# Layer 0 of a four-layer convolution kernel worked on pairs of columns, with the image laid out beforehand

## The chip, the cores and the metric

The kernel runs on one core of one Trainium2 chip, in one launch. The metric is device time in microseconds; three runs of the kernel before gave a median of 11783.54 us. One further execution was profiled, and all views below come from it. TensorE (PE, with PEld for its weight loads), VectorE (DVE), ScalarE (ACT), GpSimd (POOL) and SyncE (SP) work side by side, each through its own instructions in order. GpSimd and SyncE issue the DMAs here.

## The reference

The input `x` is 32 images of 8 channels and 256 x 256 pixels, f32. Each of four layers adds to `x` a function of its group norm (four groups of two channels). Layer 0 is by far the largest:

```python
drive = x[:, :C_OUT]                       # x here is the normalized image
grid = drive
for _ in range(15):
    mapped = 3.9 * grid * (1.0 - grid)
    local = _conv(mapped, K_local, groups=8)            # 3x3, channel by channel
    physics = 0.7 * mapped + 0.3 * local
    grid = 0.85 * physics + 0.15 * drive
cml_out = clip(grid, 0.0001, 1.0 - 0.0001)
h = relu(_conv(x, Wp, bp))                              # 3x3, 8 -> 128 channels
nca_out = sigmoid(_conv(h, Wu, bu))                     # 1x1, 128 -> 8
gin = concatenate([x, cml_out, nca_out], axis=1)        # 24 channels
g = sigmoid(_conv(relu(_conv(gin, Wg1, bg1)), Wg2, bg2))  # 3x3, 24 -> 8; 1x1, 8 -> 8
return g * cml_out + (1.0 - g) * nca_out
```

Layer 1 is a 3x3 convolution of the quantized norm, layer 2 a 3x3 convolution, layer 3 a 5x5 box filter per channel.

## The kernel before, in words

Layer 0 runs over all images first and leaves its result in DRAM (`x1_d`). Layers 1 to 3 follow in a second part, image by image.

For each image b, layer 0 has four streams of work.

`errands(b)` loads the image, takes its statistics (`bn_stats`), normalizes it in place on VectorE, stores it to a DRAM buffer with borders (`xn_d`), and loads it again in two layouts for the map (`xa`, `xb`). The other streams also read `xn_d`.

`steps(b)` is the map, the loop of 15 steps. The image lies in `state` as strips of 32 rows on 32 partitions, 4 x 36 of them, each half an image wide (130 columns with overlap). A step has three jobs s. A job is `products` (L528): for each of the three horizontal taps dx, 16 small products of a 32x32 weight with 32 x 390 columns, one for every 32x32 tile of the array, so three rounds of 16. The vertical taps and the mapped value are in the weights `wm_sb`. A job fills four of the eight PSUM banks. `take` (L543, VectorE) adds the drive and writes the new state back; a square on ScalarE (L608) makes the mapped value, since 3.9 g (1 - g) is a constant minus 3.9 (g - 0.5)^2. Every second step the layout of the strips changes sides between channel and strip, and the weights follow it. A strip has 28 rows of its own and two spare ones at each end, so rows must be passed between strips every second step: `exchange` copies columns on VectorE (L558) and issues four DMAs on SyncE for each of two groups p (L389, state<-state). The result goes to `cm_d` with DMAs of GpSimd (L385, cm_d<-xb). L482 is the square that starts an image's map, once for each p.

`hidden(n)`, four blocks n per image, is the wide convolution: eight jobs of three rounds of four products, 32 rows by 128 columns of weights over 512 columns (L690), from tiles `zx` that GpSimd loads. Each job fills four banks, which ScalarE (L697) and VectorE (L702) drain with a relu, `SHARE` = 1024 of 2048 columns on ScalarE. Two "seconds" (L725) bring 128 channels back to 8, and a sigmoid follows (L740).

`gate(n)` has three pieces (L809), for `zx`, `zc` (from `cm_d`) and `zn` (from `nn_d`): each is three rounds, one per dx, of eight products 64 x 32 over 512 columns. A 1x1 product (L837), a sigmoid and four tensor operations on VectorE close it.

The order of all this is not the order of the text. `Plan` collects the operations with a cost, a rank and a due time (`due=b + (3 * k + s) / 45` for the map, `b + LAG + ...` for hidden and gate, `LAG` = 0.6 of an image), plays them through, hands out PSUM banks through `Hold(count)`, and then emits them; each engine executes its own list in that order. So the hidden products of image b run beside the later steps of its own map and the first steps of the next one.

Of the kernel before, what the change touches and what calls it, by code (L numbers as in the profile page):

```python
# [10 lines left out]
F32 = mybir.dt.float32  # L11
# [12 lines left out]
HP, WP = H + 2, W + 2  # L24
NPX = RB * W
NCH = NPX // 512
RC = C * WP

STEPS = 15
HOP = 28  # L30
# [5 lines left out]
WT = 130  # L36
OF = 126
# [4 lines left out]
RATE = 200.0  # L42
# [4 lines left out]
SHARE = 1024  # L47
# [3 lines left out]
PAIRS = ((0,), (0, 1), (1,))  # L51
# [22 lines left out]
class Plan:  # L74
# [17 lines left out]
    def run(self):  # L92
# [33 lines left out]
        def begin(e, t):  # L126
# [25 lines left out]
            if op.size:  # L152
                moved = max(moved, t + cost) + op.size / RATE
                done = moved + HOP_US
# [40 lines left out]

def window(ap, offset, dims):
    return bass.AP(ap.tensor, ap.offset + offset, [list(d) for d in dims])
# [3 lines left out]
def kernel(  # L201
    ctx, tc, x, wm, kern, kera, eye32, wp, bp, wu, bu, wg1, bg1, wg2, bg2, w1, b1, w2, self2, near2,
    taps2, b2, w3, self3, taps3, eye, gavr, gsel, out,
):
    nc = tc.nc
    B = x.shape[0]
# [18 lines left out]
    x1_d = [dram.tile([P, NPX], F32, name=f"x1_d{b}") for b in range(B)]  # L225
    x3_d = [dram.tile([C, H, W], F32, name=f"x3_d{b}") for b in range(2)]
# [66 lines left out]
    with ExitStack() as es:  # L293
# [12 lines left out]
        wm_sb = const(wt, wm, [P, 10, 3, 32], "wm_sb")  # L306
        kern_sb = const(wt, kern, [P, 36, 9], "kern_sb")
        kera_sb = const(wt, kera, [P, 6, 9], "kera_sb")
        eye32_sb = const(wt, eye32, [P, 32], "eye32_sb")
# [4 lines left out]
        wg1_sb = const(wt, wg1, [P, 3, 3, 32], "wg1_sb")  # L314
# [4 lines left out]
        flat = wm_sb.rearrange("p c t m -> p (c t m)")  # L319
        nc.vector.tensor_scalar(flat, flat, -R_ * (1.0 - BETA_) * EPS_, None, ALU.mult)  # L320
        for c in range(10):
            nc.vector.scalar_tensor_tensor(
                wm_sb[:, c, 1, :], eye32_sb, -R_ * (1.0 - BETA_) * (1.0 - EPS_), wm_sb[:, c, 1, :],
                ALU.mult, ALU.add,
            )
        lift = wt.tile([P, 36], F32, name="lift")
        lifta = wt.tile([P, 6], F32, name="lifta")
        for t, k in ((lift, kern_sb), (lifta, kera_sb)):
            nc.vector.tensor_reduce(t, k, AX.X, ALU.add)
            nc.vector.tensor_scalar(  # L330
                t, t, 0.25 * R_ * (1.0 - BETA_) * EPS_, 0.25 * R_ * (1.0 - BETA_) * (1.0 - EPS_),
                ALU.mult, ALU.add,
            )
        minus = wt.tile([P, 1], F32, name="minus")
        nc.vector.memset(minus, -0.5)
        mean_sb = wt.tile([P, P], F32, name="mean_sb")
        nc.vector.memset(mean_sb, 1.0 / P)
# [3 lines left out]

        xbs = [wt.tile([P, 36, WT], F32, name=f"xb{i}") for i in range(2)]
        xa = wt.tile([P, 36, WT], F32, name="xa")
        state = wt.tile([P, 36, WT + 2], F32, name="state")
        nc.gpsimd.memset(state, 0.25)
        zero = wt.tile([P, 32], F32, name="zero")
        nc.vector.memset(zero, 0.0)  # L350


        xn_d = [dram.tile([HP, C, WP], F32, name=f"xn_d{i}") for i in range(3)]
        cm_d = [dram.tile([HP, C, WP], F32, name=f"cm_d{i}") for i in range(3)]
        nn_d = [dram.tile([HP, C, WP], F32, name=f"nn_d{i}") for i in range(3)]
        for t in (*xn_d, *cm_d, *nn_d):
            nc.sync.dma_start(window(t, 0, [[24, RC // 24], [1, 24]]), zero[0 : RC // 24, 0:24])
            nc.sync.dma_start(
                window(t, (HP - 1) * RC - 24, [[24, RC // 24 + 1], [1, 24]]),
                zero[0 : RC // 24 + 1, 0:24],  # L360
            )
            nc.sync.dma_start(
                window(t, RC - 1, [[16 * WP, P], [WP, 16], [1, 2]]),
                zero.rearrange("p (a b) -> p a b", b=2),
            )
# [4 lines left out]
        def part_of(xb, s):  # L370

            j, h = divmod(s, 2)
            whole = xb.rearrange("p s w -> p (s w)")[32 * j : 32 * j + 32, 0 : 2 * C * W]
            return whole.rearrange("p (c h w) -> p c h w", h=2, w=W)[:, :, h]

        def strips(q, s, i):


            p, u = divmod(4 * s + q, 6)
            h, v = divmod(u, 3)  # L380
            return HOP * (3 * v + i), p, h

        def pool_dma(to, src, after, size, rank=1):
            return add(
                "POOL", 0.6, lambda: nc.gpsimd.dma_start(to(), src()), after, rank, size=size  # L385
            )

        def sp_dma(to, src, after, rank=0):
            return add("SP", 0.58, lambda: nc.sync.dma_start(to(), src()), after, rank)  # L389


        stored_cm, stored_xn, free_a, free_s = {}, {}, {}, {}
        drive_b, drive_a, begun = {}, {}, {}
        zx_read, stored_nn = {}, {}

        def errands(b):

            xb, s = xbs[b % 2], {}
            plain = xb.rearrange("p s w -> p (s w)")
            old = stored_cm.get(b - 2, []) + [begun[key] for key in ((b - 1, 1),) if key in begun]  # L400
            loads = [
                pool_dma(
                    lambda i=i: part_of(xb, i),
                    lambda i=i: window(
                        x, b * C * H * W + 32 * i * W, [[W, 32], [H * W, C], [1, W]]
                    ),
                    old, 262,
                )
                for i in range(8)
            ]  # L410
            bns = []
            for c in range(C):
                def do(c=c):
                    if c == 0:
                        s["bn"] = small.tile([P, C, 6], F32, name="bn0")
                    nc.vector.bn_stats(s["bn"][:, c, :], plain[:, bass.ts(c, 512)])

                bns.append(add("DVE", 0.7, do, loads + bns[:1], 2))

            def join():  # L420
                s["mv"] = small.tile([P, 4, 2], F32, name="mv0")
                s["mean"] = small.tile([P, 4], F32, name="mean0")
                s["rstd"] = small.tile([P, 4], F32, name="rstd0")
                for g in range(4):
                    nc.vector.bn_aggr(
                        s["mv"][:, g], s["bn"][:, 2 * g : 2 * g + 2].rearrange("p a b -> p (a b)")
                    )
# [3 lines left out]
                add, slot, lambda: s["mv"], 4, lambda: s["mean"], lambda: s["rstd"], mean_sb, [a]  # L431
            )
            norms = [
                add(
                    "DVE", 0.8,
                    lambda g=g: nc.vector.tensor_scalar(
                        plain[:, bass.ts(g, 1024)], plain[:, bass.ts(g, 1024)],
                        s["mean"][:, g : g + 1], s["rstd"][:, g : g + 1], ALU.subtract, ALU.mult,
                    ),
                    [a], 2,  # L440
                )
                for g in range(4)
            ]
            old = [o for n in range(4 * (b - 3), 4 * (b - 2)) for o in zx_read.get(n, [])]
            stored_xn[b] = [
                pool_dma(
                    lambda i=i: window(
                        xn_d[b % 3], (1 + 32 * i) * RC + 1, [[RC, 32], [WP, C], [1, W]]
                    ),
                    lambda i=i: part_of(xb, i),  # L450
                    norms + old, 262,
                )
                for i in range(8)
            ]
            def queue(n):

                def sized(to, src, after, size):
                    return add(
                        "SP", 0.58, lambda: nc.sync.dma_start(to(), src()), after, 1, size=size
                    )  # L460

                return sized if b == 0 and n % 2 else pool_dma


            for p in range(2):
                loads = [
                    queue(h)(
                        lambda i=i, h=h, p=p: xa[
                            32 * i : 32 * i + 32, 18 * p + 9 * h : 18 * p + 9 * h + 9
                        ],  # L470
                        lambda i=i, h=h, p=p: window(
                            xn_d[b % 3], RC + (2 * i + p) * WP + OF * h + 1,
                            [[RC, 32], [HOP * RC, 9], [1, WT]],
                        ),
                        stored_xn[b] + free_a.get((b - 1, p), []), 150,
                    )
                    for i in range(4) for h in range(2)
                ]
                mine = slice(18 * p, 18 * p + 18)
                begun[b, p] = add(  # L480
                    "ACT", 2.25,
# [54 lines left out]
        def job(s):  # L536
            return slice(12 * s, 12 * s + 12)
# [41 lines left out]
        def steps(b):  # L579

            old = {s: [begun[b, p] for p in PAIRS[s]] for s in range(3)}
            for k in range(STEPS):
# [32 lines left out]
                elif k % 2:  # L615
                    got = [exchange(p, [squares[p], squares[p + 1]]) for p in range(2)]
                    for s in range(3):
                        for p in PAIRS[s]:
                            old[s] = old[s] + got[p]
# [913 lines left out]
```

## Time and profile before

| | us |
|---|---|
| median of 3 runs (lowest to highest) | 11783.54 (11780.98 to 11790.86) |
| profiled execution, its own time | 11818.99 |
| its span, first to last instruction | 11816.9 |
| first start of a map (L482) | 78.9 |
| layer 0 ends, about | 9948 |
| busy: PE / PEld | 10696.8 / 4839.0 |
| busy: DVE / ACT / POOL | 6725.5 / 4961.2 / 3791.6 |

A line of a group reads: source line, engine, operation, out<-in by the program's names, shapes, count | busy time and mean ns of one | idle time of the engine just before them, and what ended most of it. "PE bank" in the chain is TensorE writing PSUM. The granted clock is the share of full speed that the throttle gave TensorE; over the whole execution it was 0.954.

### The profile page before, as it was taken

To read this page: it belongs to the slowest core of one execution; us is meant where nothing else is said; L and a number is where in the kernel's file an instruction comes from. 1 tells how busy PE (TensorE), PEld (TensorE's weight loads), DVE (VectorE), ACT (ScalarE), POOL (GpSimd) and SP (SyncE) were. 2 spreads that over 40 slices of the span, in tenths; PEclk is the share of its full clock that TensorE was granted. 3 is DMA by queue.
4 is the path that set the end of the run, shared out by engine and by line. 5 is a ranking of instruction groups with operands and counts; after the bars stand their busy time and mean duration, and the time that the engine had idled before them with its cause. 6 is when DMAs were issued, how large, how long until landed. Compare 5 with 4: busy or idle time off the path is not lost.

```text
span 11816.9 us, 453849 instructions
## 1 busy us (share of the span) xinstructions
PE 10696.8 (91%) x210376; PEld 4839.0 (41%) x210376; DVE 6725.5 (57%) x9864; ACT 4961.2 (42%) x4254; POOL 3791.6 (32%) x6448
## 2 busy tenths in 40 slices
PE   5899999999999999999999999999999997888887
PEld 3444444444444444444444444444444443333332
DVE  4555556655556555555655556555555655555554
ACT  3444444444444444444444444444444443444443
POOL 2333333333333333333333333333333322000000
PEclk9999999999999999999999999999999998889888
DMA  4455555545455454454454455455555544555555
GB/s 86 111 117 117 116 117 114 118 113 113 113 115 114 107 113 111 111 113 110 113 116 109 111 114 116 110 113 118 117 117 116 115 98 111 140 152 148 152 153 125
DMA packets 505128, 1385.96 MB, mean 117 GB/s; under 512 B 144218, under 2 KB 223834, under 8 KB 487874
## 3 DMA queue, kind: packets, MB, share of 16 engines
q0 software_dynamic: 373184, 1163.33, 42.6%
q1 hardware_dynamic: 130050, 193.59, 7.4%
q8 instruction: 1651, 27.05, 1.0%
q14 instruction: 243, 1.99, 0.1%
HBM read 829.87 MB, written 335.84 MB: 99 GB/s over the span
## 4 chain that ended last, share of the span: by engine, by line
PE 76%; DMA 10%; DVE 5%; SPq 4%; issue 3%; ACT 2%; POOL 0%; DVEq 0%; ACTq 0%; POOLq 0%
PE bank L528 31%; PE bank L690 21%; PE bank L809 8%; PE bank L725 7%; DMA state<-state 6%; PE bank L1301 3%; PE bank L1194 3%; DVE state L543 2%; PE bank L837 2%; SPq L1341 2%; DMA xb<-x 2%; SPq L1039 1%; DMA out<-o 1%; SPq L389 1%; ACT state L608 1%
## 5 line engine op out<-in xcount | busy, mean ns | idle before, releaser
L528 PE MATMUL bank<-state,wm_sb 32*32 32x390 f32 x138240 | 4174.3, 513 | 595.6 <-DMA state<-state 280.0
L608 ACT ACTIVATE state<-state,minus 128x1560 f32<-128x1560 f32 x1344 | 2144.3, 1595 | 3075.2 <-DVE state L543 2868.9
L528 PEld LDWEIGHTS bank<-state,wm_sb 32*32 32x32 f32 x138240 | 2326.4, 104 | 2408.8 <-issue 1248.2
L690 PE MATMUL bank<-zx,wp_sb 32*128 32x512 f32 x24576 | 2903.9, 611 | 100.0 <-issue 44.6
L690 PEld LDWEIGHTS bank<-zx,wp_sb 32*128 32x128 f32 x24576 | 1240.7, 189 | 1676.7 <-issue 1379.6
L543 DVE SCALAR_TENSOR_TENSOR state<-bank,xb 128x1560 f32<-128x1560 f32 x672 | 1194.3, 1780 | 966.3 <-PE bank L528 898.5
L702 DVE TENSOR_SCALAR hh<-bank,bp_sb 128x1024 f32<-128x1024 f32 x1024 | 1311.8, 1281 | 747.2 <-PE bank L690 733.3
L543 DVE SCALAR_TENSOR_TENSOR state<-bank,xa 128x1560 f32<-128x1560 f32 x672 | 1196.8, 1781 | 928.3 <-PE bank L528 901.4
L697 ACT ACTIVATE hh<-bank,bp_sb 128x1024 f32<-128x1024 f32 x1024 | 1136.7, 1110 | 1226.7 <-PE bank L690 1220.5
L385 POOL DMA_DIRECT2D nn_d<-nh x512 | 313.0, 614 | 2564.0 <-ACT nh L740 2426.1
L725 PE MATMUL bank<-hh,wu_sb 128*32 128x512 f32 x8192 | 936.1, 596 | 5.6 <-ACT hh L697 4.9
L653 POOL DMA_DIRECT2D zx<-xn_d x512 | 298.9, 588 | 1529.5 <-PE bank L809 1443.3
L385 POOL DMA_DIRECT2D cm_d<-xb x1152 | 740.4, 1005 | 32.4 <-issue 11.3
L385 POOL DMA_DIRECT2D xb<-xn_d x1134 | 618.0, 552 | 242.7 <-DMA xn_d<-xb 146.7
L1233 POOL DMA_DIRECT2D zz<-z x256 | 124.9, 493 | 1437.9 <-ACT z L1206 1426.7
L725 PEld LDWEIGHTS bank<-hh,wu_sb 128*32 128x32 f32 x8192 | 242.0, 110 | 646.5 <-issue 595.3
L829 ACT ACTIVATE g<-bank,bg_sb 128x1024 f32<-128x1024 f32 x128 | 142.5, 1113 | 799.8 <-PE bank L809 799.8
L859 DVE TENSOR_TENSOR gt<-gt,ci 128x1024 f32<-128x1024 f32 x128 | 156.9, 1226 | 552.9 <-ACT gt L846 552.9
L385 POOL DMA_DIRECT2D xa<-xn_d x504 | 305.0, 611 | 511.9 <-DVE state L543 376.3
L740 ACT ACTIVATE nh<-bank,bu_sb 64x512 f32<-64x512 f32 x512 | 348.1, 680 | 271.9 <-PE bank L725 252.5
L1194 PE MATMUL bank<-x,w2i 64*32 64x512 f32 x6144 | 413.0, 600 | 1.6 <-ACT z L1206 1.0
L1301 PE MATMUL bank<-z,w3i 64*32 64x512 f32 x5120 | 352.5, 710 | 34.0 <-DVE z L1263 33.9
(151 smaller groups left out, 9231.1 us busy)
## 6 DMA issues: line engine op xcount, KB each, us to landing
zx<-xn_d POOLq DMA_DIRECT2D x512, 258.0 KB, 6.7
zn<-nn_d POOLq DMA_DIRECT2D x512, 258.0 KB, 6.3
zc<-cm_d POOLq DMA_DIRECT2D x512, 258.0 KB, 5.2
xa<-xn_d POOLq DMA_DIRECT2D x504, 146.2 KB, 7.4
xb<-xn_d POOLq DMA_DIRECT2D x1134, 65.0 KB, 2.7
zz<-z POOLq DMA_DIRECT2D x256, 260.0 KB, 5.8
xb<-in_x POOLq DMA_DIRECT2D x256, 256.0 KB, 11.7
xn_d<-xb POOLq DMA_DIRECT2D x256, 256.0 KB, 6.3
```

The costliest lines, as they stand in the source:

```text
L385: "POOL", 0.6, lambda: nc.gpsimd.dma_start(to(), src()), after, rank, size=size
L528: nc.tensor.matmul(t[32 * q : 32 * q + 32, 512 * g : 512 * g + 3 * WT].rearrange("p (i w) -> p i w", w=WT), wm_sb[part, c, dx, :], state[p ...
L543: nc.vector.scalar_tensor_tensor(to.rearrange("p (k i) w -> p k i w", i=3), t.rearrange("p (k w) -> p k w", w=512)[:, :, 0 : 3 * WT].rearr ...
L608: lambda t=t: nc.scalar.activation(t, t, AF.Square, bias=minus), [a],
L690: nc.tensor.matmul(t[:, bass.ts(i, 512)].rearrange("p (k w) -> p k w", w=W), wp_sb[part, par, dx, :], z[part, q : q + 5 : 4, dx : dx + W], ...
L697: nc.scalar.activation(hh[0][:, 0:SHARE], slot(hold)[:, 0:SHARE], AF.Relu, bias=bp_sb)
L702: nc.vector.tensor_scalar(hh[0][:, SHARE:], slot(hold)[:, SHARE:], bp_sb, 0.0, ALU.add, ALU.max,)
L725: nc.tensor.matmul(pn[32 * q : 32 * q + 32, :], wu_sb[:, 2 * (i % 2) + par, :], hh[:, bass.ts(i, 512)], start=seen[q] == 0, stop=seen[q] == 3,
L740: nc.scalar.activation(tiles["nh", n][part, 2 * r : 2 * r + 2, :], slot(hold)[part].rearrange("p (k w) -> p k w", w=W), AF.Sigmoid, bias=b ...
L809: nc.tensor.matmul(t[32 * q : 32 * q + 32, bass.ts(r, 512)].rearrange("p (k w) -> p k w", w=W), wg1_sb[part, i, dx, :], z[part, q : q + 5 ...
L1194: nc.tensor.matmul(t[32 * d : 32 * d + 32, bass.ts(h, 512)].rearrange("p (k w) -> p k w", w=W), w[part, d % 2, dx, :], z, start=dx == 0, s ...
L1301: nc.tensor.matmul(t[32 * d : 32 * d + 32, bass.ts(k, 512)].rearrange("p (i w) -> p i w", w=W), w, src[part, at : at + 5 : 4, dx : dx + W] ...
```

## The change

Layer 0 now works on pairs of columns.

**Map.** A strip is 16 rows of even and 16 rows of odd columns on its 32 partitions, 129 column pairs long, over the whole width of the image. A 3x3 convolution of one column of a pair needs pixels of two neighbouring pairs only, so each job has two rounds of products instead of three. By turns the pairs begin with an even and with an odd column (k even or odd). Strips are 14 rows apart with one spare row at each end, so the exchange comes after every step but the last. A step has two groups p of two jobs, one of three strips and one of two.

```diff
-            for dx in range(3):
+            for a in range(2):
                 for d in range(4):
                     for g in range(4):
...
-                            t[32 * q : 32 * q + 32, 512 * g : 512 * g + 3 * WT].rearrange(
-                                "p (i w) -> p i w", w=WT
-                            ),
-                            wm_sb[part, c, dx, :], state[part, at : at + 3, dx : dx + WT],
-                            start=dx == 0, stop=dx == 2,
+                            t[32 * q : 32 * q + 32, 512 * g : 512 * g + n * WS].rearrange(
+                                "p (i w) -> p i w", w=WS
+                            )[:, :, 0:wide],
+                            w, state[32 * g : 32 * g + 32, at : at + n, a : a + wide],
+                            start=a == 0, stop=a == 1,
...
+                for p in range(2):
+                    squares, jobs, takes = [], [], []
+                    for j, (i, n) in enumerate(((0, 3), (3, 2))):
+                        hold = Hold(4)
...
+                    done = [add("DVE", 0.25, mend, squares, -1)]
+                    old[p] = squares + done + exchange(p, k, done)
```

`exchange(p, k, after)` issues five DMAs on SyncE (before: four), with 8, 6 or 2 partitions outermost (before: 4), in runs of one to four strips of 520 bytes each. `mend` sets the edge columns with two small operations of VectorE. `take` and square have ranks -1 instead of 0 and 1.

**Gate.** The pieces read tiles of row pairs and column pairs, so each has two rounds of eight products instead of three:

```diff
-                    for dx in range(3):
+                    for d in range(2):
                         for q in range(4):
                             for r in range(2):
...
-            zn = load_z("zn", nn_d, n, 1, near + at_n(pieces, (n - 1, 2)))
+            zn = load_z("zn", nn_d, n, near + at_n(pieces, (n - 1, 2)))
...
-            for i, (name, loads) in enumerate((("zx", []), ("zc", zc), ("zn", zn))):
+            for i, (name, loads) in enumerate((("zg", zg), ("zc", zc), ("zn", zn))):
```

`load_z` issues eight DMAs instead of four, of 16 partitions x 8316 bytes each; `zg` is a new tile of the raw image.

**The image and its norm.** The host hands in the image in five layouts (`xsa`, `xsb` for the map, `xzx` for hidden, `xzg` and `xc` for the gate). `xn_d`, its stores and its reloads are gone. The norm is not applied to the image: `settle` and `weigh` scale the weights, biases, drives and the first square by mean and deviation of the group, once per image, and `pads` writes the mean into the borders of `zx` and `zg`.

```diff
-            norms = [
-                add(
-                    "DVE", 0.8,
-                    lambda g=g: nc.vector.tensor_scalar(
-                        plain[:, bass.ts(g, 1024)], plain[:, bass.ts(g, 1024)],
-                        s["mean"][:, g : g + 1], s["rstd"][:, g : g + 1], ALU.subtract, ALU.mult,
...
+            def weigh():
+                s["wp"] = hp.tile([P, 2, 3, P], F32, name="wpi", bufs=2)
+                nc.vector.tensor_scalar(
+                    s["wp"].rearrange("p a d m -> p (a d m)"),
+                    wp_sb.rearrange("p a d m -> p (a d m)"), s["mr"][:, 1:2], None, ALU.mult,
+                )
```

**Other edits.** `SHARE` goes from 1024 to 1536. `cm_d` and `nn_d` are planes by parity of row and column, and `cm_d` is written with 76 DMAs per image instead of 36. The result `x1_d` is stored by column parity; layer 1 loads it with eight DMAs instead of one, and reads and writes every second column where it puts the two together (`whole` on ScalarE, `rest` on VectorE). The plan's DMA sizes are now durations, from a count of pieces and their bytes:

```diff
-SHARE = 1024
+SHARE = 1536
...
-                moved = max(moved, t + cost) + op.size / RATE
+                moved = max(moved, t + cost) + op.size
...
+def moving(count, size, engines=16):
+
+    return count * (0.053 + 26.7e-6 * size) / engines
```

## The prediction

> **What bounds the kernel now.** I read the page first (slices, chain, groups), then the stretches between the starts of the images, then the chain in order of time inside one image, then what TensorE waited for. The program has two parts: layer 0 up to 9948 us, layers 1 to 3 after it.
>
> ```profile
> PE   5899999999999999999999999999999997888887
> PE 76%; DMA 10%; DVE 5%; SPq 4%; issue 3%; ACT 2%; POOL 0%; DVEq 0%; ACTq 0%; POOLq 0%
> L528 PE MATMUL bank<-state,wm_sb 32*32 32x390 f32 x138240 | 4174.3, 513 | 595.6 <-DMA state<-state 280.0
> L608 ACT ACTIVATE state<-state,minus 128x1560 f32<-128x1560 f32 x1344 | 2144.3, 1595 | 3075.2 <-DVE state L543 2868.9
> L543 DVE SCALAR_TENSOR_TENSOR state<-bank,xb 128x1560 f32<-128x1560 f32 x672 | 1194.3, 1780 | 966.3 <-PE bank L528 898.5
> L702 DVE TENSOR_SCALAR hh<-bank,bp_sb 128x1024 f32<-128x1024 f32 x1024 | 1311.8, 1281 | 747.2 <-PE bank L690 733.3
> L697 ACT ACTIVATE hh<-bank,bp_sb 128x1024 f32<-128x1024 f32 x1024 | 1136.7, 1110 | 1226.7 <-PE bank L690 1220.5
> ```
>
> TensorE (PE) is busy nine tenths in every slice of layer 0, and the chain that ended last is 76% TensorE. A record of the map product is half of one f32 matmul. The last column of the map row is idle time of TensorE: 595.6 us in all, 280.0 of it waiting for the exchange of rows (state<-state).
>
> The stretches (columns: length, then busy time of PE, PEld, DVE, ACT, POOL, granted clock, DMA share, GB/s):
>
> ```profile
> 4931.00:9546.00 4615.00, 4320.06 (x89209) 1995.80 (x89192) 2710.58 (x3346) 1961.75 (x1592) 1700.74 (x2881) 0.97 0.50 113
> 9948.00:11817.00 1869.00, 1490.55 (x20174) 565.78 (x20173) 948.93 (x2731) 782.01 (x868) 176.39 (x326) 0.87 0.57 144
> L482 ACT ACTIVATE state<-xa,minus x64: 2228/2238/2258, 78.9 to 9547.8; 128x2340 f32<-128x2340 f32 x64
> ```
>
> The third line (the source line that starts the map, two per image) gives the period: (9547.8 - 78.9) / 31 = 305 us per image. The first stretch holds 15 images of 307.7 us: TensorE 288, VectorE (DVE) 181, ScalarE (ACT) 131, GpSimd 113 us each. So TensorE sets the pace, and only 20 us per image are idle.
>
> Inside an image, the chain in order of time (start, length):
>
> ```profile
> 5097.77 7.89 PE bank L809 x144
> ...
> 5203.41 5.36 PE bank L690 x48
> 5208.78 8.03 PE bank L528 x269
> ...
> 5222.98 10.33 DMA state<-state
> ```
>
> Three map jobs in a row take 8.03 us, so one costs 2.68; a hidden job also 2.68 (5.36 for two); a gate, three pieces, 7.89, or 2.63 a piece. The exchange line is one that TensorE did stand still for.
>
> **Part 1: fewer products.** Before, 45 map jobs per image (15 steps of 3), each three rounds of 16 small products over 390 columns: 45 x 2.68 = 120.6 us. After, 60 jobs (15 steps, two groups p, two jobs each), each two rounds, over about 387 columns in the first job and 258 in the second. A round of 390 takes 2.68 / 3 = 0.893 us, so the first job is 2 x 0.89 = 1.79, say 1.80. The second has no row. A gate round of 512 columns takes 0.877, at most 1.713 ns a column; 390 columns explain 0.668 of the 0.893, and 0.225 is fixed. Lower end, columns alone: 2 x 258 x 1.713 = 0.88 us. Upper end, a round that does not shorten: 1.79. With the fixed part kept it is 1.33; I take 1.40, a little for the change between more jobs. Sum: 30 x 1.80 + 30 x 1.40 = 96.0, so -24.6 us per image (ends -40 and -13).
>
> The row behind the upper end is 96 records in 2.68 us, 28 ns each. The page "TensorE: Matmul & The Clock Gate" of the Trainium skill (section on the 56 ns gap) says that matmul starts never come closer than about 25 ns. By that rule a job of 64 records could not fall under 1.6 us, and the gain would be about 190 us less. The trace's records speak against it for small tiles: within a round the starts lie 16 to 17 ns apart, and the rest of the round is waiting.
>
> Gate: 12 pieces per image go from three rounds to two, 2.63 to 1.75 us: -10.5. The hidden products (32 jobs) and their seconds (8 of 3.57) keep their number and shape. Part 1 is -35.1 us per image, all of it on the engine that sets the pace.
>
> **Part 2: the draining of PSUM.** A map job holds four of eight banks until VectorE has taken it: 1.78 us and some 0.2 of hand-over. Before, the job in the other half ran 2.68 us and covered that. After, the second job runs 1.40 behind a take of 1.78, so whoever wants the first half next waits about 2.0 - 1.4 = 0.6 us, 30 times per image: 18 us if nothing fits between, 0 if pieces of the gate, which already hold their banks, or the other half fill it. I take 12, nearer the upper end, since two of three TensorE jobs of an image need four banks. The Trainium skill says the same in general ("TensorEngine Tiling (Array Packing)", section PSUM Bottleneck: tiling speeds up TensorE, not the evacuation of PSUM). It gives no price; taken strictly, the 18 us would stand, 190 us more in all.
>
> The draining engines: takes go from 45 x 1.78 = 80.1 to 30 x (1.78 + 1.24) = 90.6 us (1036 of 1560 elements scaled on the same row). The relu split moves from 1024 to 1536 on ScalarE: VectorE 32 x (1.28 - 0.69) = -19, ScalarE 32 x (1.57 - 1.11) = +15. The mending of edge columns (28 x two operations of 0.18, against 28 copies of 0.18) is +5; the clip and its zeroing +2; normalizing the image -3; new weights, biases and pads +5. VectorE stays near 181 us, ScalarE goes from 131 to about 150 (squares 42 x 1.595 to 28 x (1.595 + 1.12): +9, fewer sigmoid calls -5). In a period of 280 us these are 65% and 54%: not the bound, but queues get longer, which is in the 12.
>
> **Part 3: the exchange.** Before, 14 per image (two groups, every second step) of four DMAs; after, 28 of five. SyncE needs 0.577 us per issue: 140 x 0.577 = 81 us per image, and nothing else waits on its queue after the first image. From the first issue to the landing of the last packet the trace has 3.6 us in quiet, 4.6 in the median of lone exchanges, 8.6 at three quarters and 12.3 at 95 of 100. Every DMA used four engines; the new ones have eight or six partitions outermost. For five I add one issue: 4.2 in quiet, about 9 loaded. A cycle of one group then is: job 1.80, hand-over 0.1, takes 1.78 and 1.24, square 1.12, mend 0.4, exchange 4.2 to 9: 10.6 to 15.5 us. The period leaves 280 / 15 = 18.7. Before, two steps took at least 16.1 of products, 1.8 + 1.6 + 0.4 and the exchange of both groups (14.5 from its first issue at 5218.84 to the landing above), 34 of 41 us. So the slack grows, and the 280.0 / 32 = 8.75 us of standing shrink; I take -4 (ends -8.75, and above nothing the rival below).
>
> **Part 4: loads.** Gone are the normalized image's store to DRAM and its reloads; the image comes in five layouts instead. My count is 33.9 MB moved per image before and 39.4 after; at 280 us that is 141 GB/s, as layers 1 to 3 already reach (144). GpSimd issues 192 DMAs per image before, 208 after: 36 cm stores of 1.0 us become 76, still some 150 of 280 us. The loads are issued ahead and hidden by the hidden products; if that cover goes, a late zc piece stops a gate, 4 times per image by some us. I put 0 on it (0 to +5). Start (79 us) and layers 1 to 3 (eight x1 loads for one, strided writes of the same size) 0; strides that cost would touch ScalarE's 1.05 and VectorE's 0.67 us rows, 0 to +60 us.
>
> **Sum.** -35.1 + 12 - 4 = -27.1 us per image, x 32 = -867. The profiled execution took 11819.0 us (span 11816.9); 11819 - 867 = 10952. It lay 35 above the median of the runs, so the median becomes about 10920.
>
> **Rivals.** A: the drain takes most of it. PSUM waits at 18, the second job at 1.79 (+11.7), exchange waits unchanged: -35.1 + 18 + 11.7 = -5.4, -173 us: 11610. For it: VectorE must drain 3.0 us for every 3.2 of map product. Against: the starts 17 ns apart, and half the stream is not map.
>
> B, slower: the step chain becomes the bound. The exchange now stands in every step; with the DMA share rising from 0.50 towards 0.64 (0.50 x 39.4 / 33.9 x 307 / 280), it may sit at the trace's 12.3 us. Then 6.5 + 12.3 + 3 of waiting behind other jobs on PE and ACT is 21.8 a step, x 15 = 327 us per image, +20 x 31 = +610: about 12400. It decides from 307.7 / 15 = 20.5 us a step, that is, from an exchange (with waits) over 14 us. For it: the 95th hundredth exists already. Against: the median is 4.6, and eight engines share what four carried.
>
> C: all of it is had. No PSUM waits, no exchange waits: -35.1 - 8.75 = -43.9, -1400: 10380.
>
> **How the numbers follow.** Forecast (10400 to 11250) 0.58, A (11250 to 11750) 0.22, B 0.14, C 0.06. The range is 10380 to 11700: it takes in A and leaves out B and the extremes of C. A measurement of this kernel can tell 0.2%, 24 us. Faster by more: 0.58 + 0.06 + 0.20 of A = 0.84; within: 0.02; slower: 0.14.
>
> **What would show it.** The start line of the map 278 us apart per image; two jobs of a group in about 3.2 us; gate pieces of 1.75; idle of PE put down to takes of VectorE, new and near 12 us per image, and less than 8.75 to state<-state; DVE busy near 181 and ACT near 150 per image. Wrong if second jobs last 1.7 or more (A), if most of PE's idle is state<-state and the period is over 307 (B), or if layers 1 to 3 differ from 1869 by over 60.

## The result, and the profile after

The changed kernel took 11956.2 us (median of 4, 11950.4 to 11969.6) against 11786.5 us (median of 4) for the kernel before: ratio 1.0146, interval 1.0128 to 1.0163. It is slower by 1.5%; the forecast was 10920, faster, with a range up to 11700. The profiled execution took 11955.2 us (span 11953.3).

From the page after, the row of TensorE in 40 slices and the groups that answer to those of before:

```profile
PE   6788989888888888888888888888988556666556
L564 PE MATMUL bank<-state,wma_sb 32*32 32x387 f32 (+1 forms) x65536 | 1860.7, 456 | 282.3 <-DVE state L587 101.4
L564 PE MATMUL bank<-state,wmb_sb 32*32 32x384 f32 x57344 | 1623.5, 449 | 236.9 <-DMA state<-state 94.1
L666 ACT ACTIVATE state<-state,edge_sb 128x1556 f32<-128x1556 f32 (+3 forms) x1792 | 2426.8, 1375 | 2545.2 <-DVE state L587 2227.5
L824 DVE TENSOR_SCALAR hh<-bank,bi 128x512 f32<-128x512 f32 x1024 | 764.5, 747 | 779.1 <-PE bank L810 774.8
L818 ACT ACTIVATE hh<-bank,bi 128x1536 f32<-128x1536 f32 x1024 | 1576.5, 1540 | 1053.4 <-PE bank L810 1053.2
L1367 PE MATMUL bank<-xb,w2i 64*32 64x512 f32 x2048 | 232.9, 699 | 870.6 <-DMA xb<-x 870.6
```

and, from the kernel before, the group that answers to the last one:

```profile
L1194 PE MATMUL bank<-xb,w2i 64*32 64x512 f32 x2048 | 211.4, 606 | 29.3 <-DMA xb<-x 29.3
```

The map's rows did what was meant: 3484 us for 4174. But layers 1 to 3, the last seven slices of before at 7 and 8, are now the last nine, at 5 and 6. The borders' rows say why: TensorE stood 870.6 us for the border rows of layer 2 (xb<-x), where it had stood 29.3 us.

The stretches (length; busy PE, PEld, DVE, ACT, POOL; clock; DMA share; GB/s), 15 images of layer 0 and then layers 1 to 3, and the line that starts the map:

```profile
4626.00:8938.00 4312.00, 3839.36 (x79170) 1758.17 (x79170) 2716.01 (x4156) 2242.44 (x1681) 1786.87 (x3119) 0.97 0.52 140
9399.00:11953.00 2554.00, 1526.95 (x20174) 538.42 (x20172) 956.01 (x2732) 817.38 (x868) 320.06 (x551) 0.78 0.49 105
L518 ACT ACTIVATE state<-xa,f x64: 2507/2526/2538, 64.6 to 8948.9; 128x2560 f32<-128x2560 f32 x64
```

An image of layer 0 now takes 4312 / 15 = 287.5 us (307.7 before), with TensorE busy 256. Layer 0 ends at 9399 instead of 9948: 549 us were won. Layers 1 to 3 take 2554 instead of 1869, with almost the same busy times: 685 us were lost. 685 - 549 = 136 is the whole difference of the two spans.

Inside layers 1 to 3, TensorE in order of time (start, length, what; in brackets the idle time ahead of it):

```profile
10521.12 2.81 PE L1367 MATMUL bank<-x,w2i 64*32 64x512 f32 x48 [0.84 <-DVE u L278]
10542.99 1.91 PE L1367 MATMUL bank<-xb,w2i 64*32 64x512 f32 x2 [19.05 <-DMA xb<-x]
10553.08 1.10 PE L1367 MATMUL bank<-xb,w2i 64*32 64x512 f32 x7 [8.18 <-DMA xb<-x]
...
10559.07 8.75 PE L1474 MATMUL bank<-z,w3i 64*32 64x512 f32 x150
10568.05 8.81 PE L1474 MATMUL bank<-zz,w3i 64*32 64x512 f32 x158
```

TensorE starts layer 2 of an image, stands 19 and 8 us for its borders, and only afterwards does layer 3 of the image before (L1474), whose lines show no wait of their own. Each engine works through its list in order. In the kernel before the same pieces stand the other way round:

```profile
10739.50 11.42 PE L1301 MATMUL bank<-z,w3i 64*32 64x512 f32 x160 [0.98 <-DVE z L1263]
10750.73 8.80 PE L1301 MATMUL bank<-zz,w3i 64*32 64x512 f32 x160
10759.36 2.32 PE L1295 MATMUL bank<-zz,w3i 64*32 64x256 f32 x10
```

There layer 3 (22 us) comes first, and the borders land behind it.

### The profile page after: what moved, and what is told of

Same layout as the page of the kernel before. It is cut to its first block, busy times and chain, and to the rows that moved or that the text cites. A ratio compares the mean times of both kernels' runs of the same rounds, so it can differ in the third digit from the quotient of the medians.

```text
span 11953.3 us, 421615 instructions
## 1 busy us (share of the span) xinstructions
PE 9758.7 (82%) x189064; PEld 4300.9 (36%) x189064; DVE 6753.8 (57%) x11601; ACT 5595.9 (47%) x4448; POOL 4136.7 (35%) x7211
## 5 line engine op out<-in xcount | busy, mean ns | idle before, releaser
L666 ACT ACTIVATE state<-state,edge_sb 128x1556 f32<-128x1556 f32 (+3 forms) x1792 | 2426.8, 1375 | 2545.2 <-DVE state L587 2227.5
L810 PE MATMUL bank<-zx,wpi 32*128 32x512 f32 x24576 | 2916.0, 619 | 400.0 <-DVE state L587 181.5
L564 PE MATMUL bank<-state,wma_sb 32*32 32x387 f32 (+1 forms) x65536 | 1860.7, 456 | 282.3 <-DVE state L587 101.4
L818 ACT ACTIVATE hh<-bank,bi 128x1536 f32<-128x1536 f32 x1024 | 1576.5, 1540 | 1053.4 <-PE bank L810 1053.2
L810 PEld LDWEIGHTS bank<-zx,wpi 32*128 32x128 f32 x24576 | 1283.5, 192 | 1848.1 <-issue 1234.7
L587 DVE SCALAR_TENSOR_TENSOR state<-bank,xa 128x1552 f32<-128x1552 f32 (+1 forms) x896 | 1336.8, 1499 | 970.2 <-PE bank L564 938.9
L564 PE MATMUL bank<-state,wmb_sb 32*32 32x384 f32 x57344 | 1623.5, 449 | 236.9 <-DMA state<-state 94.1
L587 DVE SCALAR_TENSOR_TENSOR state<-bank,xb 128x1556 f32<-128x1556 f32 (+1 forms) x896 | 1328.3, 1503 | 712.0 <-PE bank L564 639.8
L564 PEld LDWEIGHTS bank<-state,wma_sb 32*32 32x32 f32 x65536 | 964.8, 104 | 1204.7 <-issue 445.3
L564 PEld LDWEIGHTS bank<-state,wmb_sb 32*32 32x32 f32 x57344 | 884.8, 104 | 982.4 <-issue 397.7
L1367 PE MATMUL bank<-xb,w2i 64*32 64x512 f32 x2048 | 232.9, 699 | 870.6 <-DMA xb<-x 870.6
```

What stands on the lines that cost most here:

```text
L564: nc.tensor.matmul(t[32 * q : 32 * q + 32, 512 * g : 512 * g + n * WS].rearrange("p (i w) -> p i w", w=WS)[:, :, 0:wide], w, state[32 * g ...
L587: nc.vector.scalar_tensor_tensor(drive if k == STEPS - 1 else strips(state, p, i, n, k % 2, wide), t.rearrange("p (k w) -> p k w", w=512)[ ...
L666: nc.scalar.activation(t, t, AF.Square, bias=edge_sb[:, 4:5])
L810: nc.tensor.matmul(t[:, bass.ts(q, 512)].rearrange("p (k w) -> p k w", w=W2), f["wp"][part, par, dx, :], z[part, of, 4 * v : 4 * v + 4, at ...
L818: nc.scalar.activation(hh[0][:, 0:SHARE], slot(hold)[:, 0:SHARE], AF.Relu, bias=f["bi"][:, 0:1],)
L1367: nc.tensor.matmul(t[32 * d : 32 * d + 32, bass.ts(h, 512)].rearrange("p (k w) -> p k w", w=W), w[part, d % 2, dx, :], z, start=dx == 0, s ...
```

## The experiments

**The theory** for the 685 us is the order: the planner writes one static list per engine from its own costs, and the eight entries for the load of x1 made it write another. **The rivals** are the other edits in that stretch: strided accesses, and short DMAs in place of one long one.

**one_load.** The eight DMAs stay, but as one entry of the plan:

```
-  out[k].append(add("POOL", 0.62, do, at_b(x1_used, b - 2) + out[0][:1],
-                    size=moving(128, 2048)))          # for each of 4 x 2 pieces
-  return out
+  a = add("POOL", 0.65, do, at_b(x1_used, b - 2), size=10.485)   # do issues all 8
+  return {k: [a] for k in range(4)}
```

> Against the changed kernel: in layers 1 to 3 the planner is told of the load of x1 as one entry (0.65 us on POOL, 10.485 us of transfer), which issues the same eight DMAs; all else of these layers, the strided accesses too, is as in the change. (The state is kept as two tiles of 20 rows and the banks as two tiles of four banks: the same instructions.) Theory, the order: with eight entries the plan lets layer 1 start on the first quarter of x1 and then puts layer 2's products right behind layer 1's, ahead of layer 3's of the image before, so TensorE stands some 20 us per image for the borders (xb<-x) that were hidden behind layer 3; one entry brings the order of the kernel before back. Then the stretch of layers 1 to 3 falls from 2554 us to 1870 to 1910 and the wait of PE for xb<-x from 870 us to under 60; the whole to about 11270 us (11230 to 11320), and layer 0 keeps its 9399. Rival, the strides: the strided bf16 writes of ACT and the short DMAs make layer 1 slower, and the plan's order only follows them: the stretch stays over 2450 us and the whole at 11850 or more.

Measured: 11655.7 us, ratio 0.9861 (0.9838 to 0.9883). Layers 1 to 3 came back to 1901 us, as the theory says. But layer 0, which the plan's edit doesn't touch, ended at 9749 instead of 9399. So two things had been changed, and the division of the tiles, meant to be neutral, was not.

**one_load_alone.** The same edit without the division.

> The edit of one_load by itself: the load of x1 as one entry of the plan, state and banks as one tile each, as in the changed kernel. In one_load layers 1 to 3 came back to 1901 us as the order theory says, but layer 0 ended at 9749 us instead of 9399, with ScalarE's and VectorE's parts of the relu waiting for each other (269 and 189 us in ten images). If the division of the banks into two tiles did that, layer 0 ends here at 9400 (within 30) and the whole takes 11300 us (11250 to 11350), some 4% under the kernel before. If the one load moved layer 0 in some way, or the 11956 us run had a lucky layer 0, it stays near 11650.

Measured: 11313.2 us, ratio 0.9555 (0.9522 to 0.9588): 4.5% under the kernel before. Layer 0 ends at 9414. Its stretch of layers 1 to 3 and its row for the borders:

```profile
9414.00:11326.00 1912.00, 1505.17 (x20174) 580.57 (x20173) 969.07 (x2732) 818.22 (x868) 320.58 (x551) 0.87 0.63 141
L1362 PE MATMUL bank<-xb,w2i 64*32 64x512 f32 x2048 | 209.7, 608 | 35.3 <-DMA xb<-x 35.3
```

The wait fell from 870.6 to 35.3 us with the strides and all eight DMAs in place. That settles the rivals for the whole kernel.

**split_in_before.** The other way round: the eight entries go into the kernel before, and with them a wait that the change also has (the last line: layer 1's products wait for the readers of the `x2` of two images before).

```
-  return add("POOL", 0.65, do, at_b(x1_used, b - 2), size=2097)
+  out[k].append(add("POOL", 0.62, do, at_b(x1_used, b - 2) + out[0][:1], size=171.7))
...
-  a = add("ACT", 1.1, shift, [loaded] + ...
+  a = add("ACT", 1.1, shift, loaded[k] + ...
-  "PE", 0.9, ... conv3(slot(h), i), near,
+  "PE", 0.9, ... conv3(slot(h), i), near + at_b(x2_used, b - 2),
```

> Against the kernel before: only the load of x1 in layers 1 to 3 becomes eight DMAs that are eight entries of the plan, each quarter of layer 1 waiting for its two, and the products of layer 1 wait for the readers of the x2 of two images before, as in the changed kernel; layer 0, the layout and the contiguous accesses stay. Theory, the order: layers 1 to 3 are written out in the changed kernel's order and cost about as much more there: 2554 instead of 1869, so about 12470 us in all (12300 to 12600), with PE waiting 700 us or more for xb<-x. Rival, the strides or the layout: neither is in this kernel, so it stays within 60 us of 11786.

Measured: 12488.3 us, ratio 1.0561 (1.0531 to 1.0592). The stretch of layers 1 to 3 and the borders' row:

```profile
9975.00:12498.00 2523.00, 1527.00 (x20174) 539.77 (x20172) 946.65 (x2731) 778.95 (x868) 304.52 (x550) 0.78 0.47 107
L1203 PE MATMUL bank<-xb,w2i 64*32 64x512 f32 x2048 | 232.7, 700 | 842.5 <-DMA xb<-x 842.5
```

The same stretch, the same wait, without any of the change's layout. Read job by job from the traces, TensorE's order in layers 1 to 3 is the same in split_in_before as in the changed kernel, and the same in one_load_alone as in the kernel before. So the cause is shown from both sides: the entries, with that wait, are enough for the loss, and taking the entries away ends it while the wait stays. Whether the entries would do it without the wait was not run.

**Kernels of 12 images.** To look at single prices, the next eight kernels do 12 images and were each run once. The first, twelve, is the change as it is; the others have at most one edit in layer 0 and one in layers 1 to 3, two stretches that don't overlap. The period of layer 0 is (start of map 12 - start of map 3) / 9; the period of layers 1 to 3 goes from spread to spread (the product with near_sb, one per image), images 2 to 11.

> The changed kernel on the first 12 of the 32 images; the other 20 are left out. It is the measure for the other kernels of 12 images: the maps should start 286 us apart as in the whole kernel, layer 0 end about 461 us after the last map's start, so at about 3675 us, and layers 1 to 3 take 80 us per image: about 4630 us in all.

| kernel | layer 0: maps 3 and 12 at | period | layers 1 to 3, per image |
|---|---|---|---|
| twelve | 575, 3178 | 289.2 | 75.6 |
| twelve_short_take | 561, 3114 | 283.7 | 61.7 |
| twelve_no_exchange | 557, 3079 | 280.2 | 74.3 |
| twelve_two_three | 578, 3238 | 295.6 | 60.0 |
| twelve_zx_first | 582, 3302 | 302.2 | 60.8 |
| twelve_no_cm_stores | 575, 3180 | 289.4 | 75.6 |
| twelve_zx_on_sp | 592, 3178 | 287.3 | 61.1 |
| twelve_two_banks | 597, 3307 | 301.1 | 58.8 |

twelve took 4627 us. Its layer 0 agrees with the whole kernel's same maps, (3188 - 581) / 9 = 289.7, so differences of half a microsecond say nothing. (Whole kernels, images 2 to 31 of layers 1 to 3: 56.4 before, 77.4 after, 57.8 in one_load_alone.)

**twelve_short_take.** `take(b, k, p, i, min(n, 2), slot(h))`, the same for the square; and `every = [o for k in range(4) for o in out[k]]; return {k: every for k in range(4)}`.

> The changed kernel on 12 images (the others left out), with two edits in different stretches. Layer 0: of the three rows of a group's job 1 only two are taken from PSUM and squared, which leaves out a fifth of the map's VectorE and ScalarE work (the third row is computed on TensorE and not used); plan and order are the same. If the drain of PSUM is what TensorE waits for in layer 0 (13.8 us per image at the take's line), most of that wait goes: a period of 274 to 280 us instead of 286. Rival, the exchange's DMAs or late loads set the step: the period stays within 3 us of 286. Layers 1 to 3: eight entries for the load of x1 as in the change, but every quarter of layer 1 waits for all eight. If the early start of the first quarter is what turns the order round, these layers return to about 58 us per image (700 us for 12); if the splitting itself costs it, they stay at about 80 (950 us).

The period of layer 0 fell by 5.5 us, a little less than expected, and TensorE's waits for the take at its three largest groups (hidden and both map rows) fell from 156 to 77 us in 12 images. TensorE's order in layer 0 is the same as in twelve. So the drain of PSUM is a real price, though the edit shortens the squares on ScalarE too, and the run doesn't part the two. Layers 1 to 3 came back to 61.7 though x1 still had eight entries. So it is the early start of layer 1's first quarter that turns the order round, not the splitting.

**twelve_no_exchange.** The exchange's entries issue nothing; qh and x2 are accessed in one piece (`[W2, 2], ..., [1, W2]` for `[1, 2], ..., [2, W2]`).

> The changed kernel on 12 images (the others left out), two edits in different stretches. Layer 0: the DMAs of the exchange between steps aren't issued, so the copied rows of the strips are stale from the first step on; their entries stay in the plan, and the order is the same. The exchange's own wait was 4.6 us per image: if that is its price, the period falls from 289 us (starts of maps 3 to 12 of twelve) to 284 to 286; if its waits only stand in front of others (VectorE's take comes late anyway), by less than 2; if it also costs through SP or the DMA engines' share, by 8 or more. Layers 1 to 3: ACT writes qh, and VectorE reads and writes x2, in one piece of 128 columns instead of every second column (the columns are then in another order than the products suppose). The order theory expects no change: 950 to 990 us for 12 images as in twelve (978). The rival, the strides: back to 700 to 800.

The period fell by 9.0, more than the 68 us of waiting in 12 images (5.7 each) that the rows put down to state<-state. TensorE's own records shrank too: the two map groups were busy 1246 us instead of 1309, 5.2 per image, and other waits took a part of all this back. Why the products run longer beside the exchange no run here tells. Layers 1 to 3 went from 75.6 to 74.3 us: the strides are not the 20 us.

**twelve_two_three.** `enumerate(((0, 2), (2, 3)))` for `((0, 3), (3, 2))`, one entry for x1, and the contiguous accesses.

> The changed kernel on 12 images (the others left out). Layer 0: a group's step begins with the job of two rows and ends with that of three (it was three, then two); the clipping and the stores of cm follow. The take of the first job is then over sooner and the square of the long one is last: if PSUM's drain is what TensorE waits for, the period moves from 289 us by 2 to 5 either way; I expect 286. Layers 1 to 3: one entry for the load of x1, and contiguous accesses as in twelve_no_exchange: the price of the strides in the good order. I expect 760 to 790 us for 12 images, and at most 25 us less than in twelve_short_take (783), which has the strides in that order.

A miss: 6.4 us slower, beyond the 2 to 5 expected and to the other side. It can't be read as a price of the drain: in the traces TensorE's order in layer 0 differs from that of twelve nearly from the start, so the edit changed far more than the order of two jobs. In the good order the contiguous accesses gave 60.0 us per image, where the strided ones gave 58.8 to 61.7: the strides have no price that these runs can tell.

**twelve_zx_first.** `moving(8 * count, 516, 8), 2` as size and rank of the stores of cm; one entry for x1.

> The changed kernel on 12 images (the others left out). Layer 0: the 76 stores of cm per image get a later rank on POOL's queue, so that the loads of zx, of which TensorE waited 4.6 us per image and 17 us in the tail behind some 43 us of these stores, are issued ahead of them. Theory: the period falls from 289 us to 283 to 286 and the tail after the last map's start from about 450 us to 435 or less. Rival: PSUM's drain takes the time as soon as the loads are there, or the gate then waits for cm (zc): the period stays within 2 us of 289. Layers 1 to 3: one entry for the load of x1 with the strides kept: 780 to 800 us for 12 images.

A miss: 13 us slower. The zx wait went, but the gate then stood for cm, as the rival had it, and more than that moved: in the traces TensorE's order in layer 0 is another, from about the second image on. Its rows for the gate's second piece:

```profile
L954 PE MATMUL bank<-zc,wg_sb 64*32 64x512 f32 x1536 | 121.0, 659 | 50.4 <-DMA cm_d<-xb 36.2 <-DMA zc<-cm_d 14.2
```

**twelve_no_cm_stores.** The entries of the stores stay in the plan and issue nothing.

> The changed kernel on 12 images (the others left out); the 76 stores of cm per image aren't issued, so that the gate's loads read an image of zeros. Their entries stay in the plan, and the order is the same. Theory: these stores, some 43 us of POOL's queue per image, make the loads of zx late, and that is the wait of 4.2 to 4.6 us per image at the line of zx's pads: the wait falls from 50 us in 12 images to under 15, the period from 289 us (maps 3 to 12) to 284 to 286, and the tail after the last map's start from 448 us to 430 or less. Rival: PSUM's drain takes the time over, and the period stays within 2 us of 289. If it falls by 8 or more, the stores cost through the DMA engines too. Layers 1 to 3 are as in the change (about 980 us).

A miss, and a useful one: period and zx wait (50.1 us for 49.9) stayed, and the tail hardly moved (445 us for 453, from the last map's start to the last gate). Without the stores GpSimd stood still instead, ahead of the load of `st` (the next image's statistics, one buffer), which waits for VectorE's bn_stats:

```profile
POOL st L412 <- DVE bn L419: 679.0, 26, 42.9
```

But it is not a load that TensorE waits for there. The wait is named for the pads (L781 here), the small operation of VectorE that writes the mean into the borders of `zx`. VectorE and TensorE in order of time, at one of these waits:

```profile
1534.75 0.51 DVE L685 TENSOR_SCALAR state<-state,edge_sb 128x20 f32<-128x20 f32 x2 [1.53 <-ACT state L666]
1535.17 1.28 DVE L419 BATCH_NORM_STATS2 bn<-st 128x6 f32<-128x512 f32 x2
1536.37 0.23 DVE L781 TENSOR_SCALAR zx<-zero,mr 128x32 f32<-128x32 f32 x1
1536.65 12.05 PE L812 MATMUL bank<-zx,wpi 32*128 32x512 f32 x96 [5.09 <-DVE zx L781]
```

The tile's second load was issued at 1521.98, and the loads of zx around it landed 4.8 to 9.9 us after their issue. VectorE came to the pads without a pause, from the mending (L685) and the bn_stats (L419) that stand ahead of them in its list. So it is in eight of the nine zx waits of this run, 40 of the 50 us. In the changed kernel, too, the pads follow the bn_stats in 25 of 26 zx waits, but there many loads land only just before. So earlier loads alone don't end this wait: the place of the pads in VectorE's list, which the plan wrote, keeps it.

**twelve_zx_on_sp and both_mended.** `nc.sync.dma_start(tiles["zx", n]...)` and `"SP", 0.58` for `"POOL", 0.62`, with one entry for x1; first on 12 images, then on all.

> The changed kernel on 12 images (the others left out), with the loads of zx issued by SyncE instead of GpSimd, and one entry for the load of x1. In twelve_zx_first a later rank for the stores of cm took the zx wait away but gave 302 us, with the gate waiting for cm. Here the stores keep their place and the loads don't stand behind them. Theory: the zx wait goes and the period is 284 to 287 us. Rival: a load of zx that waits for its buffer holds the exchange's DMAs behind it on SyncE, whose waits grow from 5.7 us per image to 10 or more: 290 to 296. If it helps it goes into a whole kernel.

> The changed kernel, all 32 images, with the load of x1 as one entry of the plan (as in one_load_alone, 11313 us) and the loads of zx issued by SyncE (as in twelve_zx_on_sp, where the period was 287.3 us against 289.2). If the 1.9 us hold over 31 images: 11250 us (11200 to 11300), some 0.5% under one_load_alone and 4.8% under the kernel before. If the twelve images were chance: 11310 within 30.

The zx wait vanished, but the edit did more than move loads: the plan wrote those pads some 50 us earlier into VectorE's list, clear of the bn_stats, and moved a few of TensorE's jobs. The period of 12 images fell by 1.9 us, a little less than expected; TensorE's waits for the exchange rose from 5.7 to 6.3 us per image. The whole kernel took 11307.3 us, ratio 0.9547 (0.9524 to 0.9570), no different from one_load_alone's 0.9555, as was expected if the gain in 12 images was chance. Over the same maps 3 to 12 both whole kernels need 289.7 us per image. A wait of 4.6 us per image was gone and no time that these runs can tell was won. Other waits grew: those for the take from 428 us in one_load_alone to 515 us.

**twelve_two_banks.** The division that had spoiled one_load, by itself: `bank = [psum.tile([P, 2048], ...) for i in range(2)]`.

> The changed kernel on 12 images (the others left out), with PSUM's banks kept as two tiles of four banks instead of one of eight (the same instructions), the state in one tile, and one entry for the load of x1. In one_load, which had banks and state divided, layer 0's period was 297 to 300 us and the two halves of the relu waited for each other. If the division of the banks does it, the period is 296 to 302 here and those waits are there again; if that of the state does it, it is 289 as in twelve.

301.1 us: the division of the banks does it. TensorE's order in layer 0 is that of twelve. What VectorE's half of the relu waits for in this kernel, then in twelve:

```profile
DVE hh L826 <- ACT hh L820: 559.4, 326, 11.2
```

```profile
DVE hh L824 <- PE bank L810: 323.4, 199, 9.7
```

In twelve both halves of the relu wait for the product and start together; here VectorE's half waits for ScalarE's. The products, takes and relus are the same, so the waits written between them are likely to differ; that was not looked into.

## Why the prediction was wrong, by its own steps

**The step that failed** is in Part 4: "layers 1 to 3 (eight x1 loads for one, strided writes of the same size) 0", with 0 to +60 for strides. The two operations it looked at were indeed cheap: with the good order the whole stretch costs 1912 - 1869 = 43 us more, inside those 60. What it did not ask is whether the order stays. The prediction took the plan's list as given and costed the edits inside it. But the list is made from the entries, and seven more of them, that let layer 1 begin earlier, put layer 3 behind the first part of layer 2. A likely reason, which no run shows, is that the planner's costs for the border transfers are small: 0.7 us of SyncE, four transfers of 1.95 us and a hop of 2.5, about 11 us by its own numbers. In the profile SyncE alone needed 10.17 us to issue the four, and the second of TensorE's waits ended at 10553.08, 27.7 us after the start of the first issue:

```profile
10525.41 10.17 SPq L1205 DMA_DIRECT2D xb<-x  x4
```

The prediction's text named "layers 1 to 3 differ from 1869 by over 60" as a sign of error; it gave that case no chance among the rivals and no price. Its only slower rival, B, was another mechanism, in layer 0.

**Part 1** held in its durations. Pairs of jobs of one group took 3.20 and 3.19 us (1.80 + 1.40 were put down), a second job 1.22 to the next start (5612.98 to 5614.20; 1.40), and gate pieces start 1.75 and 1.72 us apart (1.75):

```profile
5602.34 1.96 PE L954 MATMUL bank<-zg,wg 64*32 64x512 f32 x32 [0.91 <-DVE state L587]
5604.09 1.94 PE L954 MATMUL bank<-zc,wg_sb 64*32 64x512 f32 x32
5605.81 1.94 PE L954 MATMUL bank<-zn,wg_sb 64*32 64x512 f32 x32
...
5612.98 1.50 PE L564 MATMUL bank<-state,wmb_sb 32*32 32x256 f32 x64
5614.20 0.83 PE L564 MATMUL bank<-state,wma_sb 32*32 32x387 f32 x2
...
5637.18 3.20 PE L564 MATMUL bank<-state,wma_sb 32*32 32x387 f32 x128
5641.56 3.19 PE L564 MATMUL bank<-state,wmb_sb 32*32 32x384 f32 x128 [1.18 <-DVE state L587]
```

That second job is 64 records in 1.22 us, 19 ns apiece. The page "TensorE: Matmul & The Clock Gate" of the Trainium skill (section on the 56 ns gap) has no start under about 25 ns. The records of these small tiles lie closer; but a record is half of an f32 matmul, and whole ones start 38 ns apart. Rival A is out with that, and B, with a period of 288 us, as well. (B's own sum was a little off: 19.3 x 31 is 598, not 610.) TensorE's busy time per image (images 5 to 28, overlapping records counted once) fell by 31.4 us, from 288.0 to 256.6, where the prediction had 35.1: the map by 24.3 (24.6), the gate by 8.7 (10.5).

**Part 2**, +12 of waiting for the take: the rows that name L587 come to 181.5 + 101.4 + 80.1 + 45.0 + 14.7 = 422.7 us, 13.2 per image, against 3.5 before (72.6 + 39.7 in 32 images): +9.7. VectorE at 2716 / 15 = 181 and ScalarE at 149.5 us per image are as forecast (181 and 150).

**Part 3**, -4 for the exchange: 147.4 / 32 = 4.6 after, 8.75 before: -4.1. But twelve_no_exchange shows that its price is 9 us, so a wait named in the rows is not the whole price of a step.

**Part 4's loads**, 0 to +5: the zx wait was 147.3 / 32 = 4.6, but for another reason than a late load alone (the place of the pads in VectorE's list), and no time was won when it was gone.

Together layer 0's period fell by 19.2 us (24 images) where the sum had 27.1: 3.7 less in the products, and idle time up by 12.2 where 8 was forecast, the zx wait among it. Then the end: from the last map's start to the end of layer 0 it takes 461 us, 402 before, which cost 59 more, where nothing was put; two waits of 17 and 16 us, for `zx` and `zg`, stand in it. For layer 0 alone the sum was too good by 867 - 549 = 318 us, and the kernel would still have been faster; the sign was lost in layers 1 to 3. With their order mended the change gains 4.5% (one_load_alone), some 525 us of 11786, where the sum had 867.

## What to carry to other kernels

Where a planner writes the order, an edit that adds entries or loosens a wait can rewrite the list of every engine. Compare the order of TensorE's work before and after, in every stretch that the diff touches, and not only the cost of each operation. A plan that starts something earlier can be slower on the chip; a model that has a transfer too cheap, here 11 us for 28 in the trace, can't see it. And the price of a wait is known only when it is taken away: 4.6 us of zx were worth nothing that the whole kernel shows, 5.7 of exchange were worth 9. Look also at what stands ahead in the list of the engine that a wait names: the zx wait was named for an operation that came late because of its place in VectorE's list.

## What the runs showed that was not expected

- Standing still makes the work behind it slower too. The stretch of layers 1 to 3 ran at a granted clock of 0.78 with the long waits and 0.87 without them, and a record of the borders' product took 699 ns in the mean with them, 608 without (one_load_alone). In the 21 us of the first wait the clock was 0.63, and 0.80 in the 38 us after:

```profile
10521.00:10542.00 21.00, 2.81 (x48) 0.81 (x48) 8.94 (x27) 4.78 (x5) 4.75 (x8) 0.63 0.64 124
10542.00:10580.00 38.00, 28.84 (x428) 9.68 (x436) 9.60 (x22) 12.21 (x11) 2.00 (x4) 0.80 0.33 75
```

  The page "TensorE: Matmul & The Clock Gate" of the Trainium skill (section "What's actually happening") has the clock fall back after an idle window of about 3.4 us. The rows agree in the direction.
- SyncE took 0.7 to 5.5 us to issue one of the border DMAs of 363 to 387 KB, 2.5 us in the median (10.17 us for the four shown).
- The same instructions with PSUM's banks in two tiles instead of one cost 12 us per image; the two halves of a relu no longer started together.
